# Two transformer layers on one core: the second layer's attention taken batch by batch, and most of its mixing moved beside the first layer's last experts

## The chip, the cores and the metric

The kernel runs on one core of a Trainium2 chip. The metric is the device time in microseconds of one launch. Three runs of the kernel before gave 2106.94, 2106.09 and 2102.88 us, with a median of 2106.09. The core has five engines that each work through their own queue of instructions in order: PE (matrix products, with weight loads counted apart), DVE (elementwise work, reductions, scans), ACT (functions), POOL (elementwise work) and SP, which here only issues transfers between the chip's large memory and the core's own.

## What is computed

The input holds 8 batches of 512 tokens with 128 channels. Layer 0 has, side by side, a causal attention with 16 heads and a state-space scan, then a feed-forward part and a mixture of eight experts and a shared one. Layer 1 has a banded attention and a mixing part. Cut to what the change touches:

```python
h = _layernorm(x, axis=-1) * (1 + ca) + sa                 # layer 1
x = x + ga * _L1_attn_ref(h, Wq, bq, Wk, bk, Wv, bv)
h = _layernorm(x, axis=-1) * (1 + cb) + sb
x = x + gb * _L1_ffn_ref(h, W_r, W_k, W_v, mu_r, mu_k)

def _L1_attn_ref(val, Wq, bq, Wk, bk, Wv, bv):
    seq_len, bsz, embed = val.shape                        # 8, 512, 128
    x = jnp.swapaxes(val, 0, 1)
...
    mq = jnp.swapaxes(q.reshape(seq_len, bsz, heads, d), 0, 1)
...
def _L1_ffn_ref(x, ...):
    x_prev = jnp.concatenate([zeros, x[:, :-1, :]], axis=1)
    xr = mu_r * x + (1 - mu_r) * x_prev
    xk = mu_k * x + (1 - mu_k) * x_prev
    return sigmoid(xr @ W_r.T) * (square(relu(xk @ W_k.T)) @ W_v.T)
```

In layer 1's attention the 512 tokens of one batch fall into 8 blocks of 64, and a token attends to the 8 tokens that stand at its place in these blocks. The results of batch s go to the tokens 8u+s of all batches. So one second attention needs one finished batch of layer 0 and gives one token in eight of every batch. The mixing of a token needs that token and the one before it; so once seven of the eight second attentions are done, seven tokens of each eight can be normalised and six can be mixed; the last waits for the eighth, and the first needs the last of the eight before.

## The kernel before

All activations are held with channels on the 128 partitions and 512 tokens along the row, in `xT` (8 x 512). Layer 0 is written as generators that yield after each small piece of work, with a cost. `weave` takes several generators, each with its total cost and the share of the iteration that it is to fill, and always continues the one that is furthest behind. PE, ACT and DVE execute the pieces in exactly this order; the order on POOL and SP is made by the scheduler.

Iteration b of the main loop weaves: the attention of batch b (`attention`), its scan (`ssm_scan`), the head and scan inputs of batch b+1, and `finish(b-1)`, which is the feed-forward part (`tail`, with the layer norms ln2 and lnb), `routing`, and the nine experts of batch b-1 (`experts`). Each expert has a first half of four products with four evictions on ACT (lines 897, 901) and a second half of four products and one eviction (lines 912, 920). The last update of `xT` for a batch is line 927.

`layernorm` (line 236) takes three rounds: the mean by a product and a subtraction; the squares on ACT, the variance by small products, and the power -0.5 on POOL (line 258); then a product that spreads it over the partitions (line 263), a multiplication and the scaling on ACT.

`attention2(sp)` (line 288) works on a pair of batches, 64 places of each on the partitions. It has two layer norms (lnc), eight products of 128x384 for q, k and v (line 299), eight products on POOL with eight sums on DVE for the scores (lines 327 and 317), a softmax, and eight products on POOL with eight sums ("gathers") on DVE for the values (lines 364 and 357). Each gather is stored by a transfer. The pairs 0 and 1 run in iterations 3 to 6, the first half in the odd and the second in the even one. Pair 2 starts in iteration 7 and ends in the last weave, beside `finish(7)`. Pair 3 runs alone after it. Then the stored rows of all pairs are loaded, transposed (line 991) and added into `xT`, and `mixing(b)` runs for all eight batches, two at a time.

Of the kernel before, what the change touches and what calls it, by code (L numbers as in the profile page):

```python
# [12 lines left out]
ALU = mybir.AluOpType  # L13
# [59 lines left out]
def kernel(  # L73
# [63 lines left out]
    own = const.tile([P, NG + NDI * DS + 10], F32, name="own")  # L137
    qb_s = own[:, 10 : 10 + NG]
    A_sb = own[:, 10 + NG :].rearrange("p (c n) -> p c n", c=NDI)
# [96 lines left out]
    def layernorm(dst, src, scale, bias, name, lane, cost=0.9):  # L236

        mps = mm_tile(f"{name}_m")
        nc.tensor.matmul(mps, lhsT=mean_w, rhs=src, start=True, stop=True)
        d = lnp.tile([P, T], F32, tag=f"ln_d{lane}", name=f"{name}_d")  # L240
        nc.vector.tensor_sub(d, src, mps)
        yield cost
        sq = lnp.tile([P, T], F32, tag=f"ln_s{lane}", name=f"{name}_s")
        nc.scalar.activation(sq, d, AF.Square)
        yield cost

        vps = mm_tile(f"{name}_v")
        for j in range(NTT):
            nc.tensor.matmul(
                vps[:, j : j + 1],  # L250
                lhsT=sq[:, j * P : (j + 1) * P],
                rhs=mean_w[:, 0:1],
                start=True,
                stop=True,
            )
        sd = lnp.tile([P, NTT], F32, tag=f"ln_r{lane}", name=f"{name}_r")
        nc.vector.tensor_scalar(sd, vps[:, :NTT], EPS, None, ALU.add)
        nc.gpsimd.tensor_tensor(sd, sd, mhalf, ALU.pow)
        yield cost

        rps = mm_tile(f"{name}_rb")
        for j in range(NTT):
            nc.tensor.matmul(
                rps[:, j * P : (j + 1) * P],
                lhsT=sd[:, j : j + 1].to_broadcast([P, P]),
                rhs=ident,
                start=True,
                stop=True,
            )
        nc.vector.tensor_mul(d, d, rps)  # L270
        yield cost
        if len(dst.shape) == 3:
            d = d.rearrange("p (a b) -> p a b", a=dst.shape[1])
# [5 lines left out]

    U = T // NB  # L280
    wb_sb = const.tile([P, NWB], F32, name="wb_sb")
# [6 lines left out]
    def attention2(sp, at, nb=1):  # L288

        hT = at.tile([P, NB, 2, U], F32, tag="pr", name=f"hT{sp}", bufs=2)  # L290
        for k in range(2):
            b = 2 * sp + k
            yield from layernorm(
                hT[:, :, k, :], xT[:, b, :], mod(1, 1, b), mod(1, 0, b), f"lnc{b}", SECOND
            )
        qkv = at.tile([P, NB, 3, C], F32, tag="qkv", name=f"qkv{sp}", bufs=1)
        for i in range(NB):
            ps = mm_tile(f"qkv{sp}_{i}")
            nc.tensor.matmul(
                ps[:, : 3 * C],  # L300
                lhsT=hT[:, i, :, :].rearrange("p s u -> p (s u)"),
                rhs=cwb("qkv"),
                start=True,
                stop=True,
            )
            nc.vector.tensor_add(
                qkv[:, i, :, :].rearrange("p k c -> p (k c)"), ps[:, : 3 * C], crow("qkv_b")
            )
            yield 0.7
        yield from paced(attended(sp, at, nb, qkv))  # L310

    def attended(sp, at, nb, qkv):

        sc = at.tile([P, NB, NB, H1], F32, tag="sc", name=f"sc{sp}", bufs=1)
# [10 lines left out]
        for i in range(NB):  # L325
            pr = at.tile([P, NB, C], F32, tag="pr", name=f"pr{sp}_{i}", bufs=2)
            nc.gpsimd.tensor_mul(  # L327
                pr, qkv[:, :, 1, :], qkv[:, i, 0, :].unsqueeze(1).to_broadcast([P, NB, C])
# [4 lines left out]
            yield 0.5  # L333
# [3 lines left out]
        s3 = [P, NB, NB, H1]  # L337
        mx = at.tile([P, NB, H1], F32, tag="mx", name=f"mx{sp}", bufs=1)
# [3 lines left out]
        yield 0.5  # L342
        yield 0.5
        nc.scalar.activation(sc, sc, AF.Exp, scale=scale)
        nc.scalar.activation(mx, mx, AF.Exp, scale=-scale)
        sm = at.tile([P, NB, H1], F32, tag="sm", name=f"sm{sp}", bufs=1)
# [6 lines left out]
        kept = dram.tile([P, NB, C], F32, tag=f"ao{sp}", name=f"kept{sp}", bufs=1)  # L353
        def gathered(last):
            i, pr = last
            ao = at.tile([P, C], F32, tag="ao", name=f"ao1_{sp}_{i}", bufs=2)
            nc.vector.tensor_reduce(ao, pr.rearrange("p j c -> p c j"), AX.X, ALU.add)
            nc.sync.dma_start(out=kept[:, i, :], in_=ao)

        last = None  # L360
        for i in range(NB):
            pr = at.tile([P, NB, C], F32, tag="pr", name=f"pv{sp}_{i}", bufs=2)
# [3 lines left out]
                qkv[:, :, 2, :].rearrange("p j (h d) -> p j h d", d=D1),  # L366
# [5 lines left out]
            yield 0.5  # L372
        gathered(last)
        at2.append(kept)
# [10 lines left out]
    with ExitStack() as l0:  # L385
        psc = l0.enter_context(tc.tile_pool(name="psc", bufs=2, space=PSUM))
        pacc = l0.enter_context(tc.tile_pool(name="pacc", bufs=1, space=PSUM))
# [392 lines left out]
        def tail(b, h):  # L780
# [3 lines left out]
            yield from layernorm(h2, h, cv("ln2_w"), cv("ln2_b"), f"ln2{b}", REST, 1.4)  # L784
# [25 lines left out]
            yield from layernorm(hm, xT[:, b, :], mod(0, 4, b), mod(0, 3, b), f"lnb{b}", REST, 1.4)  # L810
# [143 lines left out]
        with tc.manual_schedule(engines={mybir.EngineType.PE, mybir.EngineType.Activation, mybir.EngineType.DVE}):  # L954
            behind, second = None, None
            for b in range(NB):
# [5 lines left out]
                if b >= 3 and b % 2:  # L962
                    second = attention2((b - 3) // 2, a2)
                if b + 1 < NB:
                    parts.append((head(b + 1), 9.5, 0.1, 0.55))
                if second:

                    parts.append((some(second, 19), 15.1 if b % 2 else 9.2, 0.0, 1.0))
# [215 lines left out]
```

## Time and profile before

| what | us |
|---|---|
| profiled execution | 2110.14 |
| its span, first to last instruction | 2108.3 |
| PE busy | 1617.5 (77%) |
| DVE busy | 1460.7 (69%) |
| POOL busy | 1044.1 (50%) |
| ACT busy | 941.2 (45%) |
| mean granted clock of PE | 0.869 |
| ACT table loads, 171 of 1.283 each | 219 |

Busy shares are means over stages with different limits. A row of the profile's timeline gives the start and the duration, the engine, the line, what is written and read, and in brackets how long the engine stood idle before it and what ended that. A fp32 product of 512 columns is two instructions on PE, which in a row follow each other 0.43 us apart. A row of transfers gives the time from issue to landing: 2.0 us for the stored rows of 64 KB (line 358), 3.3 for a pair's loads of 512 KB, 2.7 for an expert's weights and 3.2 for the row of routing weights spread over the partitions.

### The profile page before, as it was taken

What the parts mean: (1) busy time and instruction counts of PE and PEld (TensorE: products, weight loads), DVE (VectorE), ACT (ScalarE), POOL (GpSimd) and SP (SyncE); (2) the same over time, 40 slices, a digit from 0 to 9 for tenths busy, and PEclk for the clock granted to TensorE, in tenths of its full rate; (3) what the DMA queues carried; (4) which work ended last, traced back from release to release, by engine and by line L of the source; (5) the groups of instructions that cost most, each with busy time, mean ns of one, the idle gap of its engine ahead of it and who ended that gap; (6) DMA issues with size and microseconds to landing.
All of it is one profiled execution on the core that took longest, in us unless ns stands there. A gap on an engine that the chain in (4) does not pass through costs nothing. (4 is left out here: it accounts for less than half of the span.)

```text
span 2108.3 us, 22151 instructions
## 1 busy us (share of the span) xinstructions
PE 1617.5 (77%) x8408; PEld 766.9 (36%) x8408; DVE 1460.7 (69%) x1718; ACT 941.2 (45%) x1275; POOL 1044.1 (50%) x570
## 2 busy tenths in 40 slices
PE   4765868987889778876879778876888768869537
PEld 3332333333334334333334333333333333333323
DVE  2797678656874688479995777569995678335465
ACT  2522536453555455452535545453544546424113
POOL 1566345534571546266582546356583546344444
PEclk9677879997999789987989889997889889979769
DMA  2210113121222122121222112121222113103101
GB/s 100 82 65 21 52 58 97 60 75 52 91 70 77 50 65 86 46 67 55 92 64 81 45 62 90 45 72 40 91 64 87 40 65 96 46 15 111 40 20 40
DMA packets 64105, 135.78 MB, mean 64 GB/s; under 512 B 7128, under 2 KB 19552, under 8 KB 63872
## 3 DMA queue, kind: packets, MB, share of 16 engines
q1 hardware_dynamic: 63520, 132.03, 19.7%
q10 hardware_dynamic: 288, 1.93, 0.3%
q8 instruction: 66, 1.08, 0.2%
q0 software_dynamic: 192, 0.42, 0.1%
q14 instruction: 39, 0.32, 0.1%
HBM read 129.50 MB, written 4.85 MB: 64 GB/s over the span
## 5 line engine op out<-in xcount | busy, mean ns | idle before, releaser
L746 POOL TENSOR_TENSOR hs<-hs,bc 128x1024 f32<-128x1024 f32 x128 | 375.7, 2935 | 130.9 <-DVE hs L742 75.4
L742 DVE TENSOR_TENSOR_SCAN hs<-da,hs 128x512 f32<-128x512 f32 x256 | 422.7, 1654 | 4.9
L897 PE MATMUL e<-hm,we 128*128 128x512 f32 x576 | 309.6, 667 | 92.0 <-ACT eh L901 63.9
L719 POOL TENSOR_TENSOR xc<-xc,hs 128x512 f32<-128x512 f32 x112 | 187.4, 1673 | 263.4 <-DVE hs L718 263.4
L912 PE MATMUL e<-eh,we 128*128 128x512 f32 x576 | 264.3, 602 | 0.0
L923 POOL TENSOR_TENSOR moe<-moe,wb 128x512 f32<-128x512 f32 x64 | 100.5, 1570 | 300.5 <-DVE wb L920 300.5
L520 ACT ACTIVATE ex<-e 128x768 f32<-128x768 f32 (+1 forms) x192 | 158.1, 875 | 195.3 <-PE e L458 194.9
L482 DVE TENSOR_REDUCE mpad<-s 128x2 f32<-128x256 f32 (+3 forms) x256 | 194.9, 813 | 53.7 <-PE s L458 53.7
L901 ACT ACTIVATE eh<-e,vec_sb 128x512 f32<-128x512 f32 x288 | 186.7, 686 | 78.0 <-PE e L897 73.0
L737 DVE TENSOR_TENSOR hs<-bc,dtw 128x1024 f32<-128x1024 f32 x128 | 218.9, 1710 | 0.0
L897 PEld LDWEIGHTS e<-hm,we 128*128 128x128 f32 x576 | 109.5, 209 | 251.5 <-ACT eh L901 109.6
L450 PE MATMUL s<-kT,qT 32*128 32x128 f32 (+3 forms) x1024 | 146.0, 565 | 51.3 <-DVE kT L438 17.7
L704 ACT ACTIVATE da<-dtu,own 128x512 f32<-128x512 f32 x256 | 170.1, 716 | 5.4 <-POOL dtu L691 4.8
L450 PE MATMUL e<-qT,kT 32*128 32x512 f32 (+3 forms) x1024 | 119.4, 531 | 51.0 <-DVE qT L501 50.6
L912 PEld LDWEIGHTS e<-eh,we 128*128 128x128 f32 x576 | 108.2, 194 | 121.9 <-issue 115.4
L920 DVE SCALAR_TENSOR_TENSOR wb<-e,vec_sb,wb 128x512 f32<-128x512 f32 x64 | 47.7, 745 | 130.2 <-PE e L912 96.3
L901 ACT ACT_TABLE_LOAD x59 | 75.7, 1283 | 134.8 <-PE e L897 134.2
L520 ACT ACT_TABLE_LOAD x36 | 46.2, 1283 | 172.7 <-PE e L458 172.7
L718 DVE TENSOR_TENSOR hs<-hs 128x512 f32<-128x512 f32 x112 | 93.2, 832 | 34.2 <-POOL hs L746 34.2
L458 PEld LDWEIGHTS <-ident_b 128*128 128x128 bf16 x1024 | 62.5, 103 | 137.8 <-issue 130.7
L534 PE MATMUL av<-ex,va 128*32 128x512 f32 (+3 forms) x1024 | 107.2, 511 | 0.7 <-ACT ex L520 0.6
L327 POOL TENSOR_TENSOR pr<-qkv 128x1024 f32<-128x1024 f32 x32 | 80.6, 2532 | 50.9 <-DVE sc L317 39.3
(235 smaller groups left out, 2470.8 us busy)
## 6 DMA issues: line engine op xcount, KB each, us to landing
bc<-bc SPq DMA_DIRECT2D x128, 512.0 KB, 3.7
we<-in_w_dram SPq DMA_DIRECT2D x144, 256.0 KB, 2.7
wb<-wd SPq DMA_DIRECT2D x64, 256.0 KB, 3.2
xin<-in_x_dram SPq DMA_DIRECT2D x8, 256.0 KB, 4.1
kept<-ao SPq DMA_DIRECT2D x32, 64.0 KB, 2.0
ao<-kept SPq DMA_DIRECT2D x4, 512.0 KB, 3.3
out_dram<-xout SPq DMA_DIRECT2D x8, 256.0 KB, 2.3
wa_sb<-in_wa_dram ACTq DMA_DIRECT2D x1, 1832.0 KB
```

Of the source, the lines that this page charges most:

```text
L450: nc.tensor.matmul(tiles[i // 2][:, i % 2, c0 : c0 + n], lhsT=lhs[quadrant(i)], rhs=rhs[quadrant(i)], start=True, stop=False,)
L482: nc.vector.tensor_reduce(mpad[:, qi, 2 * pr : 2 * pr + 2, HD : HD + 1], tiles[pr][:, :, a : a + n], AX.X, ALU.max, negate=True,)
L520: nc.scalar.activation(t[:, :, :c0], tiles[pr][:, :, :c0], AF.Exp)
L534: nc.tensor.matmul(avs[g][quadrant(i), kj * P :], lhsT=va[:, kj, at : at + 32], rhs=ex[i // 2][:, i % 2, c0 : c0 + n], start=(kj == 0), st ...
L704: nc.scalar.activation(da[:, n, :], dt[c], AF.Exp, scale=A_sb[:, c, n0 + n : n0 + n + 1])
L719: nc.gpsimd.tensor_add(y, y, hs[:, 0, :])
L737: nc.vector.tensor_mul(hs, bcs[0], dtx[c].unsqueeze(1).to_broadcast([P, NN, T]))
L742: nc.vector.tensor_tensor_scan(hs[:, n, :], da[:, n, :], hs[:, n, :], 0.0, ALU.mult, ALU.add)
L746: nc.gpsimd.tensor_mul(hs, hs, bcs[1])
L897: nc.tensor.matmul(ps, lhsT=we1[:, m * P : (m + 1) * P], rhs=hm, start=True, stop=True)
L901: nc.scalar.activation(t, ps, AF.Silu, bias=cv("b1", e * NFF + m))
L912: nc.tensor.matmul(ps, lhsT=we2[:, m, :], rhs=hid[m], start=(m == 0), stop=(m == NFF - 1),)
```

## The change

Second attention is taken for one batch, `attention2(s)`. To use all 128 partitions, the 8 queries of a place are split into two halves of four on the two halves of the partitions; keys and values are made twice, by products with 64 output partitions each. Iterations 2 to 7 weave one whole second attention (batches 0 to 5). The rows are stored by two transfers per batch. The layer norms ln2 and lnb get an extra cost of 1.6 after the power, and `finish` counts 91.5 instead of 88.3, which moves where the weave puts pieces.

In the last weave, beside `finish(7)`, stand the second attention of batch 6, then the mixing of batches 0 to 3 (layer norm of 448 columns, mixing of 384). In a further weave the second attention of batch 7 stands beside the mixing of batches 4 to 7. `closing` then normalises the eighth token of all batches, and `closed` mixes the eighth and first tokens of all batches in two halves of 512 columns. Stored rows are loaded by 14 transfers for a pair of batches, issued when the pair before has done its transposes. Mixing uses a tanh instead of a sigmoid, with the factor 0.5 put into the gate, and its first scaling is on ACT instead of POOL.

```diff
-    def layernorm(dst, src, scale, bias, name, lane, cost=0.9):
+    def normalised(src, name, lane, cost=0.9, n=T, ring=mm_tile, wait=0.0):
...
+        nc.gpsimd.tensor_tensor(sd[:, :nj], sd[:, :nj], mhalf[:, :nj], ALU.pow)
+        yield cost + wait
...
+    def attention2(s, at):
+        hT = at.tile([P, 2, T], F32, tag="pr", name=f"hT{s}", bufs=2)[:, 0, :]
+        yield from layernorm(hT, xT[:, s, :], mod(1, 1, s), mod(1, 0, s), f"lnc{s}", SECOND)
...
+        for i0 in range(0, NB, 2):
+            ps = mm_tile(f"kv{s}_{i0}")
+            for i in range(2):
+                for k in range(2):
+                    nc.tensor.matmul(
+                        ps[half(k), 2 * C * i : 2 * C * (i + 1)],
+                        lhsT=hT[:, (i0 + i) * U : (i0 + i + 1) * U],
+                        rhs=cwb("qkv")[:, C:],
...
+            nc.vector.tensor_add(kv[:, i0 : i0 + 2, :, :]..., ps..., bias...)
+            yield 0.9
+        ps = mm_tile(f"q2{s}")
+        for i in range(NQ):
+            for k in range(2):
+                nc.tensor.matmul(ps[half(k), C * i : C * (i + 1)], ...)
...
-        for i in range(NB):
-            pr = at.tile([P, NB, C], F32, tag="pr", name=f"pr{sp}_{i}", bufs=2)
+        for i in range(NQ):
+            pr = at.tile([P, NB, C], F32, tag="pr", name=f"pr{s}_{i}", bufs=2)
...
-            yield 0.5
+            yield 1.6
...
+        kept = dram.tile([NB, U, C], F32, tag=f"ao{s}", name=f"kept{s}", bufs=1)
+        for k in range(2):
+            nc.sync.dma_start(
+                out=kept[NQ * k : NQ * (k + 1)].rearrange("i u c -> u i c"), in_=ao[half(k)]
+            )
...
-            yield from layernorm(h2, h, cv("ln2_w"), cv("ln2_b"), f"ln2{b}", REST, 1.4)
+            yield from layernorm(h2, h, cv("ln2_w"), cv("ln2_b"), f"ln2{b}", REST, 1.4, wait=1.6)
...
-                if b >= 3 and b % 2:
-                    second = attention2((b - 3) // 2, a2)
...
-                if second:
-                    parts.append((some(second, 19), 15.1 if b % 2 else 9.2, 0.0, 1.0))
+                if b >= 2:
+                    parts.append((attention2(b - 2, a2), 23.4, 0.0, 1.0))
...
-                    parts.append((behind, 88.3, 0.0, 1.0))
+                    parts.append((behind, 91.5, 0.0, 1.0))
...
-            weave((behind, 88.3, 0.0, 1.0), (second or (), 12.0, 0.0, 1.0))
...
-        for sp in range(NB // 2 - 1, NB // 2):
-            alone(attention2(sp, wk, 2))
...
+            def mixed_channels(name, n, cur, prev, t, r):
+                for k, mu in enumerate(("mu_r", "mu_k")):
...
+                    nc.scalar.activation(tk, prev, AF.Identity, scale=omu[:, k : k + 1])
+                    nc.vector.scalar_tensor_tensor(tk, cur, cv(mu), tk, op0=ALU.mult, op1=ALU.add)
+                yield 0.9
+                ps = l1_tile(f"ck{name}")[:, :n]
+                nc.tensor.matmul(ps, lhsT=cwb("k"), rhs=t[1], start=True, stop=True)
+                nc.vector.tensor_scalar(t[1], ps, 0.0, None, ALU.max)
+                nc.scalar.activation(t[1], t[1], AF.Square)
+                ps = l1_tile(f"cr{name}")[:, :n]
+                nc.tensor.matmul(ps, lhsT=cwb("r"), rhs=t[0], start=True, stop=True)
+                nc.scalar.activation(r, ps, AF.Tanh, scale=0.5)
+                yield 1.8
+                ps = l1_tile(f"cv{name}")[:, :n]
+                nc.tensor.matmul(ps, lhsT=cwb("v"), rhs=t[1], start=True, stop=True)
+                nc.vector.scalar_tensor_tensor(r, r, 1.0, ps, op0=ALU.add, op1=ALU.mult)
+                yield 0.9
...
+            def fetched(i0):
+                two = halves_of(ssm, "bc0", f"ai{i0}", 2)
+                for i, ai in zip((i0, i0 + 1), two):
+                    ai = ai.rearrange("p (j c) -> p j c", c=C)
+                    for s in range(LAST):
+                        nc.sync.dma_start(out=ai[half(s % 2), s // 2, :], in_=at2[s][i])
+                    fetch[i] = ai
...
+            def mixing(i, lane):
+                N = LAST * U
+                M = N - U
...
+                for j in range(LAST // 2):
+                    nc.tensor.transpose(ps[:, j * P : (j + 1) * P], ai[:, j, :], ident)
...
+                yield from layernorm(
+                    hp, xa, mod(1, 4, i), mod(1, 3, i), f"lnd{i}", lane, 0.9, N, l1_tile
+                )
+                nc.scalar.copy(x0[:, i, :], xa[:, :U])
+                nc.scalar.copy(now[:, i, 1, :], hp[:, :U])
+                nc.scalar.copy(past[:, i, 0, :], hp[:, N - U :])
...
+                yield from mixed_channels(i, M, hp[:, U:], hp[:, :M], t, r)
...
+            def pair(i, lanes):
+                both = [mixing(i + k, lanes[k]) for k in range(2)]
+                for k in range(2):
+                    yield next(both[k])
+                if i + 2 < NB:
+                    fetched(i + 2)
...
+            def through(sp):
+                yield from attention2(sp, a2)
+                fetched(0)
+            SHARE = 4
+            weave(
+                (behind, 91.5, 0.0, 1.0),
+                (
+                    chain(through(LAST - 1), *(pair(i, (MIX, SECOND)) for i in range(0, SHARE, 2))),
+                    23.4 + 11.7 * SHARE, 0.0, 1.0,
+                ),
+            )
...
+            def closing():
+                ps = l1_tile("aoT_z")
+                for j in range(NQ):
+                    nc.tensor.transpose(ps[:, j * P : (j + 1) * P], at2[LAST][:, j, :], ident)
...
+                d = yield from normalised(
+                    x7.rearrange("p i u -> p (i u)"), "lnz", SECOND, 0.9, T, l1_tile
+                )
...
+            def closed(k):
...
+                yield from mixed_channels(f"_z{k}", T, flat(now), flat(past), t, r)
...
+            weave(
+                (attention2(LAST, a2), 23.4, 0.0, 1.0),
+                *(
+                    (pair(i, (MIX, REST)), 23.4, 0.15 + 0.45 * k, 0.7 + 0.45 * k)
+                    for k, i in enumerate(range(SHARE, NB, 2))
+                ),
+            )
+            alone(closing())
+            weave((closed(0), 4.5, 0.0, 1.0), (closed(1), 4.5, 0.0, 1.0))
```

## The prediction

> **What bounds the kernel now.** I read the busy time by stage first, cutting the span where the last operation on xT (line 927) ends each iteration's expert work. Columns: stretch, length, busy time (and instructions) of PE, PE's weight loads, DVE, ACT, POOL, granted clock, DMA share, GB/s.
>
> ```profile
> 464.00:687.00 223.00, 183.42 (x993) 85.02 (x994) 153.53 (x182) 113.22 (x152) 107.63 (x57) 0.89 0.22 70
> 687.00:920.00 233.00, 190.31 (x1041) 91.59 (x1042) 161.08 (x196) 116.20 (x156) 112.83 (x62) 0.90 0.21 67
> 920.00:1165.50 245.50, 188.58 (x993) 86.86 (x992) 200.75 (x206) 114.11 (x154) 141.97 (x71) 0.87 0.22 66
> 1165.50:1401.00 235.50, 193.53 (x1041) 91.60 (x1040) 160.02 (x196) 115.80 (x156) 111.32 (x60) 0.89 0.21 67
> 1401.00:1647.00 246.00, 191.65 (x994) 88.59 (x993) 200.38 (x206) 114.53 (x154) 142.20 (x71) 0.85 0.20 65
> 1647.00:1857.00 210.00, 167.20 (x920) 76.68 (x918) 138.66 (x167) 102.32 (x136) 104.31 (x52) 0.92 0.20 62
> 1857.00:1963.00 106.00, 88.40 (x212) 40.26 (x213) 43.68 (x70) 38.58 (x55) 40.95 (x26) 0.87 0.24 70
> 1963.00:2031.00 68.00, 17.96 (x76) 12.29 (x74) 46.28 (x63) 4.95 (x7) 37.06 (x19) 0.61 0.05 18
> 2031.00:2108.30 77.30, 58.13 (x232) 32.77 (x232) 41.04 (x64) 26.11 (x41) 32.18 (x38) 0.88 0.11 34
> ```
>
> The reader is to see three kinds of stage. An iteration without second attention costs 223.0 us (first row). With a pair's normalisation and qkv it costs 233.0 or 235.5, with that pair's scores, softmax and sums 245.5 or 246.0. So a hidden pair costs 10.0+22.5 and 12.5+23.0: 34 us, 17 per batch. The last two stages, 145.3 us, have nothing beside them. The timelines of POOL, DVE and PE show that end (start, duration, engine and line, in brackets the idle time before and what ended it):
>
> ```profile
> 1986.10 18.45 POOL L327 TENSOR_TENSOR pr<-qkv 128x1024 f32<-128x1024 f32 x8 [11.37 <-DVE qkv L306]
> 2011.42 15.68 POOL L364 TENSOR_TENSOR pv<-qkv,sc 128x1024 f32<-128x1024 f32 x8 [6.87 <-DVE sc L352]
> ...
> 2021.29 7.72 DVE L357 TENSOR_REDUCE ao<-pv 128x128 f32<-128x1024 f32 x4 [0.15 <-POOL pv L364]
> ...
> 2034.09 1.97 PE L991 MATMUL aoT<-cst_sb,ao 128*128 128x128 f32 x8 [48.67 <-DMA ao<-kept]
> ```
>
> The last pair keeps POOL and DVE in turns for 66 us while PE idles 48.67 us; the gather ends at 2029.0 and PE starts at 2034.1, so store plus load cost 5.1. Last, what PE waits for in the plain iteration (first lines of its waits):
>
> ```profile
> PE e L897 <- ACT eh L901: 10.9, 8, 4.3
> PE lnb_rb L263 <- POOL lnb_r L258: 6.1, 1, 6.1
> PE lna_rb L263 <- POOL lna_r L258: 5.1, 1, 5.1
> PE e L450 <- DVE qT L501: 4.9, 2, 3.2
> PE ln_rb L263 <- POOL ln_r L258: 4.6, 1, 4.6
> ```
>
> All queues run in order, so PE stands still while a normalisation's power (POOL) is late. The chain of waits shows only the last microseconds and carries nothing here.
>
> **The main loop (iterations 1 to 7).** Iterations 2 to 7 each get one whole second attention; before, 3 to 6 held two pairs and 7 the first half of the third. Per batch the change does: one normalisation as before (PE 2.7 us: 0.86 + 0.95 + 0.95 from the spacing of its rows); 16 products of 64x256 and 8 of 64x128 instead of half of 6.87 us (the row qkv L299 x16); five evictions of 512 columns at 0.69 (row L241) instead of half of eight at 0.56, +1.2 us of DVE; half as many score products, sums and gathers as a pair, each of the same size; a softmax of half size, some 0.3 us dearer on DVE than half a full one. So 19 us of DVE per batch (1.5 + 3.5 + 4.8 + 2.5 + 7.8 is 20 with no overlap).
>
> *The 64-wide products.* The trace has no 64-column product. The nearest row is the 32-column one, rb L566: 32 instructions in 1.08 us, 34 ns apart, where one of 128 columns takes about 110 ns alone: the column groups run at once. Two halves at once make 3.4 + 0.9 = 4.3 us per batch; one after the other 8.6. [...] The row for a switch: k L434, right after 32-column products, starts its second pass 0.52 us after the first where 0.43 is usual, 0.1 us. [...] I take 4.3 and the row; 8.6 stays as the bad end.
>
> Price per batch: the score half as the trace has it, 23/2 = 11.4, plus 0.8 us per DVE microsecond added (22.5 us of time for 28 us of DVE work, summed at each row's shortest duration) on 1.5 us: 12.6. The normalisation half 11.2/2 = 5.6, times 7.0/6.1 for PE: 6.4. Sum 19.
>
> What is saved: `wait=1.6` puts more pieces of the other streams between the power and its broadcast product. In the new order of PE, a block of score products with masks (1.75 + 0.40), lna's variance (1.0) and a k/v block (0.9) stand ahead of lnb_rb, 4 of the 6.1 us; for ln2 PE's order there is as before (4.6 stays) but DVE gets a scan (1.2) ahead. The first experts stand later behind the routing, which shortens their 4.3 us wait for ACT. ACT's table loads fall from 171 to 154, of 1.28 us each. I take 5 us per iteration together: PE and DVE both stood still in these waits (DVE's own: 3.1 and 5.4 us).
>
> Sum: iteration 1: 223 to 218, -5. Iterations 2 to 6: 223+233+245.5+235.5+246 = 1183 to 5 x (223+19-5) = 1185. Iteration 7: 210 less 11 for the half pair, plus 19-5: 213. That is 0; but the gathers now run in the last quarter of each iteration, where the scan is over and DVE has slack (12.7 us busy of 23 in 664 to 687): I credit 1.3 of their 7.8 us in each of six iterations, **-8 us**. Bounds: +30 (halves serial, no slack found), -35 (waits gone, sums fully covered).
>
> **The last weave (106 us).** Before, it held the third pair's scores beside the last batch's FFN and experts. Of these 106 us, the first 36 are a chain (layer norms, FFN, routing) with PE half idle; then PE runs eighteen expert blocks back to back at 3.43 us. The change adds there batch 6's second attention and, for four batches, the layer norm of 7/8 and the mixing of 6/8 of the tokens. PE per mixing batch: mean 0.75, variance 1.0, broadcast 1.0, three products of 384 columns 1.9, seven transposes and one half 0.85: 5.5 us (spacings of L239, L249, L263, L1022, L1040, scaled by columns), 22 for four; there is no idle PE to take it. The chain: lnc6 is queued ahead of ln2's variance, power and ACT steps (about +2.5), three k/v blocks ahead of the FFN (+2.6): +5. Then a new wait: PE's transposes of batch 0 (aoT0) stand right behind the first expert's first half and need batch 6's stored rows. The gathers are interleaved with routing's small DVE operations; counted down DVE's queue from the xT update, the last gather ends about 27 us after it; store and load 5.1; so 32, where PE had its first second-half expert at 22.7. Behind the waiting transposes are all further experts: +9 us. In SP's queue the fourteen loads of the next pair wait for the same transposes, with the third expert's second weights behind them; these are needed 30 us later, so nothing. Then ACT runs in order: hp1 waits for a DVE product queued behind wb7_1, whose row needs store and load (before, DVE waited 5.57 us there and PE 1.2), with the third expert's evictions behind hp1 (about +4), and the first ck waits for copies and scalings after that expert (+4); later ones 2. Sum 22+5+9+10 = **+46**; bounds +36 and +58.
>
> **The tail (145.3 us).** It keeps one batch of second attention with four mixings beside it, then the last and first token of each eight. From the last expert product: xT 3.2, normalisation 8.5, k/v and q interleaved with two layer norms 10, four score products at 2.3 and the last sum 10.5, softmax 6 (with a 1.28 table load that now is behind two squares). Then POOL: pv, two powers, pv; DVE: four gathers 7.8 among 8 mixing operations and three pauses: 24, to 62-65. Closing: transposes, two 0.69, layer norm 5.5, three 0.69, one copy: 11.5. Closed halves: ACT 2.8, DVE 4, then ck, relu, square, cv, gates, transposes, copy: 13, and 3.7 from the last copy to the end of the span as before. Sum 92.
>
> [...] By the row, DVE grew by 47 us (153.5 to 200.8) in the even iterations for 28 of work: 19 us for 16 products, 1.2 each, 10 here. Many of these fall into pauses: I take 3. So 95: **-50**; bounds -60 and -38.
>
> **Sum.** -8 + 46 - 50 = -12 us against the profiled execution, 2110.1 (span 2108.3 and 1.8 around it): 2098. The median of the runs shown, 2106.1, is 4 lower: **2094**. Less than 0.2%, some 4 us, can't be told from no change.
>
> **Rivals.**
> A. *The expert block can't take the mixing* (slower). One mechanism: PE is full there (0.0 us idle before L912), so each wait of an in-order ACT or DVE instruction of mixing stalls experts. If every one of 9 experts loses 3 us instead of the 10 in all, the weave grows by 63, and with a tail of -42 and a loop at 0 the time is 2127. It decides from +58 in the weave. For it: the 1.2 and 1.4 us PE waits already there. Against: DVE has 62 us idle there. 0.34 with its milder forms.
> B. *The loop gains much*: waits for the powers vanish and gathers hide: loop -35, 2067. For it: 15.8 us of waits for powers per iteration. Against: DVE is busy 79 of the first 90 us of an even iteration. 0.14.
> C. *The gains and losses cancel* within 4 us (loop 0, weave 48, tail -48): 2106. 0.12.
> Forecast: 0.40. So faster 0.54, same 0.12, slower 0.34. Range from the bounds, all three terms rarely at one end: 2050 to 2132; the forecast's own 2076 to 2101.
>
> **What would show it.** Iterations of 230 to 240 us each; lnb_rb waiting under 3 us; the last weave near 152 us with PE waiting once 6 to 9 us at the first aoT; from the last expert product to the end 95 us. A wait for k/v products, an iteration over 245, or a weave over 165 makes the prediction wrong.

## The result, and the profile after

Five runs of the changed kernel gave a median of 2119.01 us (2116.8 to 2122.53); five of the kernel before, on the same chip, 2106.94. The ratio is 1.0057, with an interval of 1.0032 to 1.0081: **slower** by 12 us, where the forecast said 2094. The profiled execution took 2119.01 us, with a span of 2117.1.

The busy time by stage of the changed kernel, cut at the last update of `xT` in each iteration (now line 968), has the columns of the table before (stretch, length, PE, PE's weight loads, DVE, ACT, POOL, granted clock, DMA share, GB/s):

```profile
458.90:695.50 236.60, 193.85 (x1056) 90.71 (x1056) 177.88 (x206) 113.90 (x155) 128.68 (x66) 0.88 0.22 66
695.50:930.90 235.40, 195.96 (x1056) 91.44 (x1056) 177.52 (x206) 112.77 (x154) 126.86 (x65) 0.87 0.22 68
...
1637.50:1853.20 215.70, 171.78 (x938) 77.31 (x938) 159.84 (x178) 98.56 (x133) 118.22 (x56) 0.89 0.22 66
1853.20:2009.50 156.30, 123.72 (x398) 64.82 (x398) 60.59 (x109) 52.86 (x95) 34.52 (x23) 0.85 0.19 53
2009.50:2050.00 40.50, 27.99 (x138) 18.34 (x138) 25.61 (x32) 9.97 (x22) 12.67 (x7) 0.79 0.02 4
2050.00:2080.00 30.00, 14.46 (x48) 9.00 (x46) 20.60 (x26) 9.19 (x21) 10.30 (x6) 0.66 0.04 9
2080.00:2117.10 37.10, 17.80 (x48) 10.12 (x48) 14.72 (x25) 8.26 (x14) 1.01 (x1) 0.60 0.10 25
```

Iterations 2 to 6, each with one second attention, now last the same, 235.4 to 236.6. The last weave (fourth line shown) is 156.3 us. The last three lines are the tail, 107.6 us, and the column to look at is the clock: 0.79, 0.66, 0.60. Set beside the stages of the kernel before, which I cut anew at the same instruction in both traces:

| stage | before | after | change | forecast |
|---|---|---|---|---|
| to the end of iteration 1 | 464.3 | 458.9 | -5.4 | -5 |
| iterations 2 to 6 | 1182.5 | 1178.6 | -3.9 | |
| iteration 7 | 211.0 | 215.7 | +4.7 | |
| main loop, all three | 1857.8 | 1853.2 | -4.6 | -8 |
| last weave | 107.2 | 156.3 | +49.1 | +46 |
| tail | 143.3 | 107.6 | -35.7 | -50 |

So the loop and the last weave came out within 4 us, and the tail gave back 14 us less than the forecast said. Rows of PE from the changed kernel's timeline (start, duration, in brackets the idle time before and what ended it), the first at the start of the last weave and the others in the tail, show the first suspect:

```profile
1856.53 1.05 PE L255 MATMUL lnc_v<-cst_sb,lnc_s 128*128 128x1 f32 x8 [1.44 <-ACT lnc_s L248]
...
2012.85 1.86 PE L255 MATMUL lnc_v<-cst_sb,lnc_s 128*128 128x1 f32 x8 [1.44 <-ACT lnc_s L248]
...
2037.97 1.65 PE L1065 MATMUL ck<-mix,wb_sb 128*128 128x384 f32 x2 [6.25 <-DVE mix L1060]
...
2089.13 1.87 PE L255 MATMUL lnz_v<-cst_sb,lnz_s 128*128 128x1 f32 x8 [1.44 <-ACT lnz_s L248]
```

The same eight variance products, after the same pause of 1.44 us, take 1.05 us in the last weave and 1.86 in the tail. The second suspect stands in the groups by shape: one of DVE and one of POOL in the tail, and the same one of DVE in the last weave. A row has the count, then busy time and mean ns of one.

```profile
L1060 DVE SCALAR_TENSOR_TENSOR mix<-xa,vec_sb,mix 128x384 f32<-128x384 f32 x8 | 11.4, 1475 | 0.7 <-ACT mix L1059 0.7
L359 POOL TENSOR_TENSOR pr<-kv,q 128x1024 f32<-128x1024 f32 x4 | 9.7, 2429 | 7.5 <-DVE sc L349 4.1 <-DVE q L337 3.4
...
L1060 DVE SCALAR_TENSOR_TENSOR mix<-xa,vec_sb,mix 128x384 f32<-128x384 f32 x8 | 4.6, 616 | 9.4 <-ACT mix L1059 9.4
```

The operation that mixes a token with the one before takes 1475 ns on the mean in the tail and 616 in the last weave, and PE's 6.25 us wait above is for this very operation. The mean of the tail hides two sorts: four of its eight last 2.1 to 2.7 us, about as long as the POOL product beside them, the other four 0.60 to 0.62. In the last weave no POOL instruction runs beside any of the eight, and all last 0.61 to 0.62.

### The profile page after: what moved, and what is told of

Its sections match the earlier page's. It is cut to its first block, busy times and chain, and to the rows that moved or that the text cites. A ratio compares the mean times of both kernels' runs of the same rounds, so it can differ in the third digit from the quotient of the medians.

```text
span 2117.1 us, 22844 instructions
## 1 busy us (share of the span) xinstructions
PE 1670.0 (79%) x8762; PEld 797.5 (38%) x8762; DVE 1485.7 (70%) x1761; ACT 937.2 (44%) x1318; POOL 1027.4 (49%) x539
## 3 DMA queue, kind: packets, MB, share of 16 engines
q1 hardware_dynamic: 66816, 131.51, 20.2%
q10 hardware_dynamic: 288, 1.93, 0.3%
## 5 line engine op out<-in xcount | busy, mean ns | idle before, releaser
L938 PE MATMUL e<-hm,we 128*128 128x512 f32 x576 | 325.2, 700 | 104.8 <-DVE wb L961 38.0
L953 PE MATMUL e<-eh,we 128*128 128x512 f32 x576 | 275.1, 622 | 0.4
L776 DVE TENSOR_TENSOR hs<-bc,dtw 128x1024 f32<-128x1024 f32 x128 | 242.1, 1891 | 0.0
L938 PEld LDWEIGHTS e<-hm,we 128*128 128x128 f32 x576 | 116.2, 220 | 261.3 <-issue 99.1
L489 PE MATMUL e<-qT,kT 32*128 32x512 f32 (+3 forms) x1024 | 131.3, 568 | 76.8 <-DVE qT L540 75.6
L489 PE MATMUL s<-kT,qT 32*128 32x128 f32 (+3 forms) x1024 | 135.2, 529 | 25.2 <-DVE kT L477 15.5
L394 POOL TENSOR_TENSOR pv<-kv,sc 128x1024 f32<-128x1024 f32 x32 | 62.2, 1952 | 116.2 <-DVE ao L388 95.8
L359 POOL TENSOR_TENSOR pr<-kv,q 128x1024 f32<-128x1024 f32 x32 | 90.8, 2847 | 34.1 <-DVE sc L349 18.6
L489 PEld LDWEIGHTS e<-qT,kT 32*128 32x128 f32 x1024 | 49.6, 210 | 136.4 <-DVE qT L540 85.1
L573 PE MATMUL av<-ex,va 128*32 128x512 f32 (+3 forms) x1024 | 95.5, 463 | 0.1
```

Of the source, the lines that this page charges most:

```text
L489: nc.tensor.matmul(tiles[i // 2][:, i % 2, c0 : c0 + n], lhsT=lhs[quadrant(i)], rhs=rhs[quadrant(i)], start=True, stop=False,)
L776: nc.vector.tensor_mul(hs, bcs[0], dtx[c].unsqueeze(1).to_broadcast([P, NN, T]))
L938: nc.tensor.matmul(ps, lhsT=we1[:, m * P : (m + 1) * P], rhs=hm, start=True, stop=True)
L953: nc.tensor.matmul(ps, lhsT=we2[:, m, :], rhs=hid[m], start=(m == 0), stop=(m == NFF - 1),)
```

## The experiments

Each ran in five or more executions beside the kernel before. The stages are from the profiled execution, cut as above; "tail" runs to the end of the span. The tail's code is the same in the changed kernel, e2, e5, e8 and e13, and took 107.6 to 110.3 us there: differences under 3 us in it say nothing by themselves. The runs stood on several chips; the kernel before had medians of 2106.3 to 2107.0 us beside them, but 2111.2 beside e13 and e14, so for these two the ratio says more than the median.

| kernel | median us | ratio to before, interval | it. 1 | it. 2-6 | it. 7 | last weave | tail |
|---|---|---|---|---|---|---|---|
| before | 2106.94 | | 464.3 | 1182.5 | 211.0 | 107.2 | 143.3 |
| changed | 2119.01 | 1.0057 (1.0032-1.0081) | 458.9 | 1178.6 | 215.7 | 156.3 | 107.6 |
| e1 before + gap | 2078.68 | 0.9875 (0.9853-0.9896) | 455.7 | 1162.7 | 202.8 | 110.5 | 143.6 |
| e2 changed - gap | 2127.99 | 1.0105 (1.0083-1.0126) | 464.2 | 1174.9 | 217.6 | 160.5 | 109.7 |
| e3 SHARE 0 | 2107.5 | 1.0005 (0.9992-1.0018) | 458.3 | 1179.0 | 215.1 | 101.8 | 151.5 |
| e4 SHARE 8 | 2131.27 | 1.0121 (1.0099-1.0143) | 460.3 | 1178.6 | 215.6 | 197.4 | 76.5 |
| e5 later start | 2118.12 | 1.0055 (1.0043-1.0067) | 459.4 | 1172.5 | 214.1 | 158.4 | 110.3 |
| e6 PE filled | 2111.77 | 1.0029 (1.0017-1.0041) | 457.0 | 1178.7 | 215.4 | 156.9 | 101.3 |
| e7 PSUM | 2113.15 | 1.0024 (1.0010-1.0038) | 459.4 | 1178.7 | 215.6 | 156.3 | 101.4 |
| e8 pause | 2124.06 | 1.0085 (1.0072-1.0098) | 459.4 | 1179.3 | 215.3 | 156.8 | 110.3 |
| e9 e6 and e7 | 2106.29 | 0.9987 (0.9972-1.0003) | 458.3 | 1179.0 | 215.8 | 156.3 | 92.3 |
| e10 before, 91.5 | 2104.98 | 0.9986 (0.9968-1.0003) | 456.4 | 1179.7 | 208.5 | 111.1 | 146.2 |
| e11 before, all gaps | 2062.72 | 0.9781 (0.9755-0.9808) | 455.3 | 1145.1 | 204.3 | 109.7 | 146.3 |
| e12 e9, SHARE 0 | 2090.79 | 0.9918 (0.9895-0.9941) | 458.3 | 1179.4 | 215.6 | 101.3 | 133.9 |
| e13 changed, all gaps | 2101.31 | 0.9951 (0.9938-0.9965) | 455.6 | 1161.3 | 216.0 | 156.7 | 110.3 |
| e14 e12, all gaps | 2072.63 | 0.9811 (0.9795-0.9826) | 456.3 | 1161.5 | 215.9 | 100.9 | 136.3 |

### The tail: the clock, and DVE against POOL

My theory after the result: the tail was counted with rows of a PE at speed (the eight variance products: 1.05 us, where they took 1.86) and too little for DVE beside POOL (2.1 to 2.7 us, where undisturbed operations took 0.60 to 0.62). Its rival: the order of the woven work.

**e6_fill.** Products that nobody reads are put in PE's pauses in the tail, into the tile that the next product overwrites. The lines show the layer norm of batch 7's attention (`lnc`); `lnz` has `fill=(1, 1, 1)`, and `lnd` of batch 6 has `(0, 0, 3)`.

```diff
+    def filled(ps, n):
+        for _ in range(n):
+            nc.tensor.matmul(ps, lhsT=mean_w, rhs=wb_sb[:, : ps.shape[-1]], start=True, stop=True)
...
         mps = ring(f"{name}_m")[:, :n]
+        filled(mps, fill[0])
...
         vps = ring(f"{name}_v")
+        filled(vps, fill[1])
...
         rps = ring(f"{name}_rb")
+        filled(rps, fill[2])
...
+            fill=(2, 1, 1) if s == NB - 1 else (0, 0, 0))
...
                 ps = l1_tile(f"ck{name}")[:, :n]
+                filled(ps, {4: 4, 6: 4, "_z0": 3}.get(name, 0))
```

> The changed kernel with 21 products added in the tail that nobody reads, in TensorE's pauses (ahead of the first ck of each pair and of the last tokens, of the second pair's variance broadcast, and in the two layer norms without mixing), each in the tile that the next product overwrites. Theory 1 (a slow granted clock is what made the tail 15 us too long): the rows at half clock (1.87 for eight variance products) fall to 1.05, the tail from 107.6 to 96-101 from the last xT update, so 2107 to 2113. Theory 2 (the tail is set by DVE and POOL, and TensorE waits for them): tail 106 to 111, so 2117 to 2123.

Measured: 7.2 us less, the tail 101.3. PE's timeline of this kernel:

```profile
2011.37 1.05 PE L264 MATMUL lnc_v<-cst_sb,lnc_s 128*128 128x1 f32 x8 [0.58 <-ACT lnc_s L256]
...
2051.70 1.87 PE L264 MATMUL lnd_v<-cst_sb,lnd_s 128*128 128x1 f32 x8 [1.93 <-ACT lnd_s L256]
...
2083.81 1.05 PE L264 MATMUL lnz_v<-cst_sb,lnz_s 128*128 128x1 f32 x8 [0.58 <-ACT lnz_s L256]
```

Where a product was added just before (first and third line) the variance is back at 1.05; where none was, behind a pause of 1.93 us (second), it stays at 1.87. The whole tail, in the changed kernel and in this one:

```profile
2009.50:2117.10 107.60, 60.26 (x232) 37.45 (x232) 60.93 (x81) 27.43 (x57) 23.98 (x14) 0.69 0.05 13
2008.00:2109.30 101.30, 70.73 (x270) 39.98 (x270) 61.17 (x81) 27.36 (x57) 23.89 (x14) 0.83 0.06 13
```

PE did 21 products more, the granted clock rose from 0.69 to 0.83, and the tail got shorter, so the clock was a cause: theory 1, for about half of what was missing. At 0.83 the clock still isn't full, so 7.2 us need not be all that it costs.

**e7_psum.** For the four batches mixed in the tail ACT writes the scaled token to PSUM, so DVE reads one input from SBUF and one from PSUM.

```diff
+                    sk = tk
+                    if name in range(SHARE, NB):
+                        sk = l1_tile(f"mx{name}_{k}")[:, :n]
-                    nc.scalar.activation(tk, prev, AF.Identity, scale=omu[:, k : k + 1])
-                    nc.vector.scalar_tensor_tensor(tk, cur, cv(mu), tk, op0=ALU.mult, op1=ALU.add)
+                    nc.scalar.activation(sk, prev, AF.Identity, scale=omu[:, k : k + 1])
+                    nc.vector.scalar_tensor_tensor(tk, cur, cv(mu), sk, op0=ALU.mult, op1=ALU.add)
```

> The changed kernel in which, for the four batches mixed in the tail, ACT writes the scaled previous token to PSUM, so that DVE's product and sum there reads one input from SBUF and one from PSUM. Theory 2 (DVE and POOL hold each other off where both read SBUF): these operations fall from about 1.4 to 0.6-0.9 us beside POOL's products, the tail shrinks by 4 to 8, so 2111 to 2115. Theory 1 (the clock): no change in the time, 2117 to 2121, whatever the operations themselves do. Rival to both: the PSUM ring is short and tiles wait for it, slower by 2 to 6.

Measured: 5.9 us less. The same two groups of this kernel's tail:

```profile
L359 POOL TENSOR_TENSOR pr<-kv,q 128x1024 f32<-128x1024 f32 x4 | 9.3, 2354 | 4.1 <-DVE q L337 3.4 <-DVE sc L349 0.7
...
L1063 DVE SCALAR_TENSOR_TENSOR mix<-xa,vec_sb,mx 128x384 f32<-128x384 f32 x8 | 4.5, 609 | 1.0 <-ACT mx L1062 1.0
```

The operation falls from 1475 to 609 ns beside the same POOL products, 6.9 us for eight, and POOL's own wait for the sums (`sc`) from 4.1 to 0.7. All eight now last 0.60 to 0.61 us. The granted clock of the tail is 0.70 for 0.69, so this gain isn't the clock's. Theory 2's numbers hold as well, so neither theory alone. DVE still reads one input from SBUF here: the run shows two inputs there against one, for this operation.

**e9_fill_psum**, both edits:

> The changed kernel with both edits in the tail: the added products that nobody reads, and the scaled token in PSUM. If the slow TensorE clock and the hold-off between DVE and POOL are two separate causes, their gains add: 7 and 6 us, 13 of the 15 by which the tail missed the forecast, so 2104 to 2108. If both shorten the same wait (the first ck behind the mixed tokens), 7 to 9 together: 2110 to 2113.

Measured: 12.7 us less than the changed kernel, against 7.2 + 5.9 = 13.1 one by one, so the two gains add (in the profiled tails 15.3, against 6.3 + 6.2, which the tail's spread of 3 allows). The tail is 92.3 us, by 143.3 - 50 the forecast was 93.3. That doesn't clear the rival, the order of the woven work: no run changes it. In the changed kernel the last score product ends on POOL at 2046.33, and its sum starts on DVE 5.2 us later, behind mixing work that stands ahead of it in DVE's queue:

```profile
2043.98 2.35 POOL L359 TENSOR_TENSOR pr<-kv,q 128x1024 f32<-128x1024 f32 x1 [0.20 <-DVE sc L349]
...
2051.50 1.21 DVE L349 TENSOR_REDUCE sc<-pr 128x64 f32<-128x1024 f32 x1
```

With both edits (e9) this delay is still 5.5 us. What another order would give wasn't tried.

### Mixing beside the experts, or in the tail

**e3_share0** and **e4_share8** change one number, `SHARE = 4` to 0 and 8.

> The changed kernel with no mixing beside the last experts (SHARE 0): the last weave has the second attention of batch 6 and the first gathers alone, and all eight batches are mixed in the tail. Theory (the tail is slow because work is woven into the attention of batch 7, and each pair mixed there costs 15 to 18): last weave 156 to 118-128, tail 108 to 138-146, sum -8 to +8, so 2111 to 2127. Rival (mixing is cheap in the tail, since its engines idle there, and dear beside the experts): tail 108 to 120-128, sum about -15 to -20, so near 2100.

> The changed kernel with all eight batches mixed beside the last experts (SHARE 8): the tail has the attention of batch 7 and the closing alone. Theory (the tail lost its 15 us to mixing woven into the attention): last weave 156 to 175-185, tail 108 to 76-84, sum -12 to +5, so 2107 to 2124. Rival (the attention of batch 7 alone is what is long, by a slow TensorE clock, and mixing fills its gaps): tail 108 to 90-98, sum +5 to +19, so 2124 to 2138.

Measured: SHARE 0 is 11.5 us faster than the changed kernel and level with the kernel before, below the theory's 2111, since the last weave fell to 101.8 and not to 118; its tail, 151.5, was longer than either had it. SHARE 8 is 12 us slower: its tail of 76.5 is the theory's, its last weave of 197.4 is above what either allowed, so that its time lies in the rival's range without the rival's reason. So both expectations had mixing too cheap beside the experts. The busy time of the last weave and the tail, for SHARE 0 (first fence) and SHARE 8 (second):

```profile
1852.40:1954.20 101.80, 90.48 (x274) 42.98 (x274) 35.51 (x73) 39.90 (x57) 30.06 (x19) 0.95 0.21 61
1954.20:2105.70 151.50, 94.91 (x356) 59.82 (x356) 81.92 (x118) 44.24 (x97) 27.93 (x18) 0.69 0.09 23
```

```profile
1854.50:2051.90 197.40, 149.81 (x522) 82.16 (x522) 77.75 (x145) 69.42 (x135) 37.99 (x27) 0.86 0.16 46
2051.90:2128.40 76.50, 28.33 (x108) 16.50 (x108) 33.89 (x45) 10.57 (x17) 18.91 (x10) 0.61 0.03 7
```

A pair of batches mixed beside the experts costs 27 us for the first two pairs ((156.3 - 101.8) / 2) and 21 for the next; in the tail it costs 16 and 22. `SHARE` also sets how much of the weave batch 6's attention may fill: all of it with 0, the first third with 4. So the 27 us hold the crowding of that attention with the first steps of the weave too; no run parts the two.

Four batches beside the experts add 33 us of PE (90.5 to 123.7, at a clock of 0.85 for 0.95) and 21 of PE's waits, summed over its list of waits (9.2 to 30.7). The 33 us are not all work. In the changed kernel's weave the granted clock is 0.50 in six stretches, 47.8 us in sum, and PE is busy for 32.4 of them; with SHARE 0, whose mean of 0.95 over 101.8 us makes some 10 us at 0.50, for 8.7. If that busy time is halved, an estimate of the work at full clock, it grows from 86.1 to 107.5 us, by 21, and the other 12 are the slower clock. The largest of the waits in the changed kernel:

```profile
PE e L938 <- ACT eh L942: 6.0, 1, 6.0
PE aoT L1111 <- DMA ai<-kept: 5.0, 1, 5.0
PE ck L1065 <- DVE mix L1060: 2.9, 1, 2.9
```

**e8_gap** moves the transposes that make the second of these waits behind the first half of expert 1.

```diff
                 fetched(0)
+                for _ in range(4):
+                    yield 2.5
...
-                    23.4 + 11.7 * SHARE, 0.0, 1.0,
+                    33.4 + 11.7 * SHARE, 0.0, 1.0,
```

> The changed kernel with a pause of 10 us of weaving between the loads of batch 0's rows and its transposes, which puts these behind the first half of expert 1 instead of expert 0. Theory (the two waits ahead of the second half of expert 0, 6.0 for ACT and 5.0 for the rows, are stalls of TensorE's queue that other experts can fill): the last weave falls from 156 to 146-151, so 2109 to 2114. Rival (the experts there wait for the routing's and the mixing's DVE and ACT work, whatever the order): last weave 154 to 160, 2116 to 2123.

Measured: 2124.06, the last weave 156.8. The wait for the rows is gone from the list, and the sum of PE's waits there is 31.5 for 30.7; its head is now

```profile
PE e L938 <- ACT eh L942: 5.0, 2, 4.4
PE ck L1065 <- DVE mix L1060: 4.7, 2, 3.0
PE lnb_rb L270 <- POOL lnb_r L265: 4.2, 1, 4.2
```

The rival holds for the weave, and the time is a little above its range: the waits of the layer norm (2.3 before) and of `ck` (2.9 before) have grown in place of the one that went.

**e12_share0_both** has SHARE 0 and both tail edits, for all four pairs.

> The changed kernel with all mixing in the tail (SHARE 0) and both edits there, for all four pairs. If each pair mixed in the tail loses 3 us to the clock and 3 to DVE and POOL: 2107.5 less 18 to 24, so 2083 to 2090. If only what stands beside the attention of batch 7 does: 2107.5 less 8 to 13, 2094 to 2100.

Measured: 16.7 us less than SHARE 0, the tail 151.5 to 133.9, between the two guesses and next to the first. This arrangement beats the kernel before by 0.8%.

### The main loop

**e1_wait_alone**: the kernel before with the gap and 91.5 alone (the lines show ln2; lnb has the same gap, and the last weave the same 91.5).

```diff
-        yield cost
+        yield cost + wait
...
-            yield from layernorm(h2, h, cv("ln2_w"), cv("ln2_b"), f"ln2{b}", REST, 1.4)
+            yield from layernorm(h2, h, cv("ln2_w"), cv("ln2_b"), f"ln2{b}", REST, 1.4, wait=1.6)
...
-                    parts.append((behind, 88.3, 0.0, 1.0))
+                    parts.append((behind, 91.5, 0.0, 1.0))
```

> The kernel before with one part of the change alone: the longer gap (1.6) after the variance step of the two layer norms between attention and experts, and the expert block's length 91.5 for 88.3. Theory (as in the prediction): the gap is worth about 5 us in every iteration that has an expert block, from the second on, and nothing in the last weave: 7 times 3 to 5, so 2071 to 2085, ratio 0.984 to 0.990. Rival: the 5 us that went at the end of iteration 1 went for another reason (no second attention beside it), and the gap is worth nothing by itself: 2100 to 2112.

Measured: 2078.68. The loop falls by 36.6 us, just over the theory's upper end, and the last weave gives 3 back. **e10_pace** has only 91.5 for 88.3:

> The kernel before with 91.5 for 88.3 as the length of the expert block and nothing else: its pieces are spread by 3.5% without the gap behind the variances. Theory (the gap itself does it: other products stand between the power and its broadcast): 2102 to 2112, as before. Rival (the slower pace of the expert block does it, by another order of everything): 2078 to 2090, as with the gap.

Measured: 2104.98. The time is as before, but the loop alone fell by 13 (8 of it in iteration 1) and the last weave and tail gave 7 back; so of the 36.6 some 23 are the gap's and 13 come with the pace, roughly, as each loop was profiled once. **e2_wait_undone** takes gap and pace out of the changed kernel:

> The changed kernel without the longer gap (0 for 1.6, 88.3 for 91.5), all else as changed. Theory: the main loop loses 3 to 5 us in each of iterations 1 to 7, so 2140 to 2154; the last weave and the tail stay as they are. Rival (the gap is worth nothing by itself): 2112 to 2126, and iteration 1 ends as in the changed kernel.

Measured: 2127.99, a miss for both. Iteration 1 loses 5.3 as the theory said, iterations 2 to 6 *gain* 3.7; the rest of the 9 us stands in iteration 7 (1.9), the last weave (4.2) and the tail (2.1, within its spread). PE's waits in one iteration (the fourth) without the gap, then with it (the changed kernel):

```profile
...
PE lnb_rb L270 <- POOL lnb_r L265: 4.7, 1, 4.7
...
PE e L489 <- DVE qT L540: 4.1, 1, 4.1
PE lnc_m L242 <- DVE xT L968: 3.9, 1, 3.9
```

```profile
PE e L489 <- DVE qT L540: 9.5, 2, 7.0
PE e L938 <- DVE wb L961: 5.2, 1, 5.2
...
PE lnc_m L242 <- DVE xT L968: 3.9, 1, 3.9
```

With the gap the wait for lnb's power is gone, and the waits for `qT` and `wb` have grown by 5.4 and 4.4 (`wb` from 0.8). In sum the waits of this iteration are 41.2 without the gap and 39.3 with it, so they don't explain why the gap gains nothing: the granted clock is 0.90 without it and 0.87 with it (0.865 and 0.858 over the whole span). Why the clock fell wasn't tested. The line that both have, `lnc_m`, is a stall that the change made: the second attention's first product stands at the start of each iteration and reads the `xT` that the last expert has just updated. **e5_start** begins it at 0.06 instead of 0.0 of the iteration:

> The changed kernel with the second attention of a batch begun at 0.06 of each iteration instead of 0.0; all its work is kept. Theory: lnc's mean product, which reads the xT that the last expert of the iteration before has only just updated, stands first in PE's queue and holds it 3.9 us in each of six iterations; moved down, iterations 2 to 6 fall from 235.5 to 231-233 and the time to 2095-2105. Rival (the 235.5 is set by something else, and the stall moves on as the power's wait did with the longer gap): iterations stay at 234-237, 2113 to 2124.

Measured: 2118.12. That wait is gone from the list, iterations 2 to 6 fall by 6.1 together instead of 12 to 22, and the time is unchanged, as the rival had it. PE's waits of this iteration sum to 37.6 for 39.3. **e11_wait_all** and **e13_after_all** put the gap also into the two layer norms that open a batch, in the kernel before and in the changed one:

```diff
-            yield from layernorm(h, xT[:, b, :], mod(0, 1, b), mod(0, 0, b), f"lna{b}", MIX)
+            yield from layernorm(h, xT[:, b, :], mod(0, 1, b), mod(0, 0, b), f"lna{b}", MIX, wait=1.6)
...
-            yield from layernorm(xn, h, cv("ln1_w"), cv("ln1_b"), f"ln1{b}", MIX)
+            yield from layernorm(xn, h, cv("ln1_w"), cv("ln1_b"), f"ln1{b}", MIX, wait=1.6)
...
-                    parts.append((head(b + 1), 9.5, 0.1, 0.55))
+                    parts.append((head(b + 1), 12.7, 0.1, 0.55))
```

> The kernel before with the gap of 1.6 and 91.5, and the same gap in the two layer norms that open each batch (whose powers hold TensorE 4.9 and 4.1 us in an iteration with the gap in the other two). Theory (a wait for a power is worth its time wherever it stands): another 2 to 4 us in each of seven iterations, 2051 to 2066. Rival (the time goes to the next thing in the queue, as in the changed kernel's loop): 2072 to 2086.

> The changed kernel with the gap of 1.6 also in the two layer norms that open each batch, as e11_wait_all had it on the kernel before (there: 16 us). Theory (in the changed loop the freed time goes to other waits of the in-order queues): iterations stay at 233-237, 2112 to 2124. Rival (each covered power is worth its time here too): iterations of 231-233, 2100 to 2109.

Measured: 2062.72 and 2101.31, 16 us less than e1 and 17.7 less than the changed kernel (some 22 by the ratios): the theory holds in the old loop and the rival in the changed one. So the changed loop isn't closed to such gains; only the gap at ln2 and lnb was worth nothing in its iterations 2 to 6. The fourth iteration of e13, 232.1 us, has PE waits of 42.2 in sum, more than the changed kernel's 39.3 in 235.5, yet less PE busy time (189.8 for 196.2) at a clock of 0.90 for 0.87. Its gain shows in the clock and not in the sum of waits; why the clock was higher wasn't tested. **e14_all_share0**, the best form of the change:

> e12_share0_both (the changed kernel, all mixing in the tail, products nobody reads and PSUM there) with the gap in the opening layer norms too. Adding up: 2090.8 less what e13_after_all gains, so 2084 to 2094 by the theory (nothing to gain in that loop) and 2072 to 2082 by the rival; behind the 2062.7 of the kernel before with the same gaps in either case.

Measured: 2072.63, at the rival's lower end, as e12 less the 17.7 of e13 has it. By its median it stays 10 us behind the kernel before with the same four gaps (e11, 2062.72), the fastest kernel tried; by the ratios it is 0.3%, and their intervals overlap. In the profiled executions its loop is 29 us behind, its last weave and tail 19 ahead.

## Why the prediction was wrong

**The step that failed is the tail: "Sum 92", "I take 3", "So 95: -50".** Counted as there, from the end of the last expert product, it took 109.9 us. Its steps, each to the end of its last operation, from the timelines of the changed kernel and of e9, which has both edits of the tail:

| step | forecast | changed | e9 |
|---|---|---|---|
| `xT` | 3.2 | 3.1 | 3.1 |
| normalisation | 8.5 | 9.6 | 8.6 |
| k/v and q | 10 | 12.6 | 11.4 |
| score products and last sum | 10.5 | 20.2 | 16.3 |
| softmax | 6 | 6.0 | 6.0 |
| values and gathers | 24 | 21.6 | 16.9 |
| closing | 11.5 | 17.0 | 14.8 |
| closed halves, to the end | 23.5 | 19.8 | 17.5 |
| sum | 97.2 | 109.9 | 94.6 |

The forecast's terms add to 97.2 and not to 92, so 5 us of the miss are a wrong addition. With 100 in place of 95 the forecast is still "faster", 2099. Then two terms were mis-sized. The steps have no allowance for a slow PE, though the table of stages shows a clock of 0.61 where PE idles most of the time, and the new tail idles the same way (0.69): the layer norm of `closing`, priced at 5.5, took 8.9, and 6.7 in e9. Filling the pauses is worth 7.2 us. And DVE against POOL was put at 3, an estimate, where the row gave 10; taking it from mixing's eight operations (1475 to 609 ns each) is worth 5.9. Both are shown by runs, and with the addition they make up the 15 us that the tail missed: 5, 7, and the 3 by which 5.9 exceeds what was put. That e9 comes near the forecast's total is partly luck: the score step is still 6 us longer than forecast, behind mixing work on DVE, and the values and gathers 7 us shorter.

The miss against 2094 is some 25 us: 14 in the tail, 3 each in the loop and the last weave, and the 4 us taken off because the profiled execution of the kernel before stood above its median; that of the changed kernel is its median. Of the signs named beforehand, the iterations (235), the weave (156) and the wait at the first `aoT` (5.0 for 6 to 9) came out near; the tail alone did not.

**The last weave, +46, was right as a sum** (+49.1) and partly by luck. Against SHARE 0, whose last weave is 101.8, the mixing costs 54.5: stalls 21, where I had 24 with the chain, and PE 33 for 22. Of the 33 some 21 are work, as forecast, and 12 the slower clock, for which the forecast had nothing here either. What offset it: with the third pair's leftover gone and batch 6's attention in its place this weave is 5 us shorter (107.2 to 101.8), where I had counted additions alone. The wait of the transposes was forecast at 9 and measured as 6.0 for ACT plus 5.0 for the rows; e8 shows that taking the 5.0 away buys nothing.

**The main loop, -8, was right (-4.6) with two wrong terms that cancel.** A batch was priced at 19 us and `wait` at -5 per iteration. Without the gap (e2) iterations 2 to 6 last 235.0 on the mean, 12 above the plain 223, and the gap adds 0.7: 12.7 in all, where 19 - 5 and the credit of 1.3 for hidden gathers, which no run tests, also make 12.7. Iteration 1 ended 5.4 earlier as forecast, but e10 gives 8 there by the pace alone, so "the gap" is not shown as its cause. The `lnc_m` stall was not seen beforehand; it would have been an argument against the change, and a wrong one, since e5 takes it away and the time stays. The two 64-wide halves ran at once as assumed:

```profile
1862.77 2.81 PE L314 MATMUL kv<-wb_sb,hT 128*64 128x256 f32 x24 [0.32 <-ACT hT L284]
```

These 24 passes of 256 columns took 2.81 us; one after the other, at 0.43 us for 512 columns, they would take 5.2.

**Rival A** named the right place (the expert block can't take the mixing) and the wrong size: +63 for a measured +49; with its tail of -42 and its loop of 0 it came nearest, 2127. Rival B's loop gain of 35 exists, but on the kernel before (e1). What the whole change costs beyond its gap is the difference of e1 and the changed kernel, 40 us: the loop +32 (six whole batches of second attention in it instead of two pairs and a part), the last weave +46, the tail -36.

## What to carry to other kernels

Price a stage at the clock it will run at: here a row of PE in a chain with pauses took up to 1.8 times as long as in a busy stage (1.87 us for 1.05), and 21 products that nobody reads, put in the pauses, took 7.2 us off the time. Moving work from an idle tail into a stage that is full on one engine pays only what that tail really loses; measure both prices for one unit (here a pair: 21 to 27 us beside the experts, 16 to 22 in the tail) before building the move. Add up the terms of a forecast a second time. Test each part of a compound change alone: its smallest part, a gap of 1.6 in the weave with its pace, was worth 28 us, and all the rest on top of it cost 40.

## What the runs showed of the hardware

The same pause of 1.44 us stands before variance products of 1.05 and of 1.87 us, a factor of 1.78: the single pause doesn't decide it. In the traces of the kernel before and of the changed one every stretch of the granted clock is at 1.00 or at 0.50. Around the two slow rows at 2012.85 and 2037.97 it changes as follows in the changed kernel:

```profile
2003.59:2012.22 8.63, 4.73 (x12) 1.63 (x10) 2.19 (x3) 0.98 (x3) 1.26 (x1) 1.00 0.10 23
2012.22:2022.46 10.24, 8.26 (x33) 6.14 (x34) 3.20 (x5) 1.39 (x2) 1.02 (x1) 0.50 0.01 2
2022.46:2036.11 13.65, 9.26 (x76) 6.57 (x75) 8.88 (x13) 5.57 (x14) 5.55 (x4) 1.00 0.00 0
2036.11:2042.94 6.83, 4.97 (x8) 2.85 (x9) 5.27 (x7) 1.15 (x3) 2.91 (x2) 0.50 0.00 0
```

The second fall, at 2036.11, lies inside the pause of 6.25 us, 4.4 us after its start. The first fall, at 2012.22, lies inside the pause of 1.44 us, behind 1.1 us of PE and a pause of 3.09 before that. So the clock fell in a long pause and in a short one soon after another; what decides when it falls, no run here shows.

The operation that mixes a token with the one before took 609 ns on the mean with one of its two inputs in PSUM (e7), beside POOL's products; 1475 in the changed kernel's tail with both in SBUF, of which four ran 2.1 to 2.7 us beside these products; and 616 in its last weave, also with both in SBUF, where no POOL instruction ran beside it.
